# A four-layer graph network: layer 1's input and the small rows turned by VectorE and DRAM instead of TensorE, one statistics instruction per norm, and a mask kept in DRAM

## The chip, the cores and the metric

The kernel runs on one core of one Trainium2 chip. The metric is the device time of one execution in microseconds (us). A core has TensorE (PE, matrix products), VectorE (DVE), ScalarE (ACT), GpSimd (POOL) and SyncE (SP), which issues all DMAs here; 16 DMA engines carry them out. Every engine works through its own instructions in the order in which the program has them.

## The reference, cut to what matters

There are 64 independent graphs of N = 256 nodes with D = 256 features, and everything is float32. Four layers follow each other, and around each is a residual and a layer norm over the features:

```python
x = _layernorm(x + _L0_gnn_ref(x, adj, ...))   # 4 heads, sigmoid(q k^T) * adj, degree-normed; own layer norm
x = _layernorm(x + _L1_gnn_ref(x, adj, ...))   # 8 heads, softmax(where(adj > 0, q k^T / sqrt(32), NEG))
x = _layernorm(x + _L2_gnn_ref(x, adj, ...))   # (adj @ x + eps x) W1 + b1, rmsnorm, silu, W2 + b2  (hidden 1024)
x = _layernorm(x + _L3_gnn_ref(x, adj, ...))   # Wh = x W; softmax(where(adj > 0, leaky(s1_i + s2_j), NEG)) Wh
                                               # own layer norm, gelu
```

In layer 1, q = x Wq + bq, k = x Wk + bk, v = x Wv + bv. In layer 2, the rms norm multiplies every token's hidden row by rsqrt(mean(h^2) + 1e-6). In layer 3, s1 and s2 are Wh times the two halves of the vector a. The biases bq and bk are inputs (they hold zeros).

## The kernel before, in words

**Tiling.** A graph's 256 x 256 array is one tile of 128 partitions by 512 words: two halves n of 128 tokens each, side by side. A product that sums over features needs its operand feature-major (features on the partitions), so x has to be transposed between layers.

**A planner sets the order.** `graph` records each step of one graph as an operation with an engine, a cost, the values that it reads and writes, and for ACT work that needs a function table a turn. `Plan.order` then lays out all 64 graphs at once, picking at every step the operation that can start first by the costs written in the code, with the buffer slots of `SLOTS` as a limit. Turns go round by round: in a round the sigmoid of one graph's layer 0 is done, then the exponentials of layers 1 and 3 of older graphs, then the silu of layer 2, then the gelu of layer 3. `ROUND = 0, 2, 5, 7` says how many rounds later a graph's layer 1, 2 and 3 have their turn, and `TAIL` presses the last graphs together. So at any moment some eight graphs are under way, and PE takes matmuls of one graph while others wait for DVE, ACT or a DMA. The order that comes out is fixed in the program.

**PE's three ways of working.** Most matmuls use the whole array (mode `full`). The scores of layers 0 and 1 (L502, L582) use it in `rows`, the weighted sums of these layers and two small sums over partitions (L542, L618, L520, L680) in `columns`, so that several small products run side by side. `CHANGE` lists what the planner reckons for a change of mode. With `JOINT = 8, 58` the small sum of one graph's layer 2 (L680, columns) is joined to the first scores of another graph's layer 1 (L582, rows) in the middle rounds.

**Two ways to transpose a tile.** `transposed` (L323) uses four PE transposes of 128 x 128 into PSUM, and `copy` (L359, ACT) brings the result to SBUF. `far_transposed` uses DVE's transpose of 32 x 32 blocks (L335), writes the result to DRAM and reads it back so that the blocks land where they belong. With `in_order=True` that is four DMAs of 64 KB out (L341, pieces of 512 B) and four back (L345, pieces of 128 B); otherwise it is one of 256 KB out (L349) and four back (L351). Layer 0's result, layer 3's input (`xT3`) and layer 3's weights (`eT3`) go this way, except for the first or last few graphs (`NEAR`); layer 1's weights have a version of their own (L603, L605, L607). Layer 1's input `xT` goes through PE for every graph.

**Small rows.** A value per token that sits on the partitions has to be laid along the free axis, for all partitions alike, in three places. For layer 1's reciprocals r, PE transposes them (L625), ACT copies them (L627), and they go out to DRAM and come back spread over the partitions (L628, L631). For layer 2's rms factor, `rs` is computed on POOL (L688) and PE transposes a broadcast column into PSUM (`pr`, L693, two transposes). For layer 3's s2 the same is done from `v3` (L731).

**Norms.** `stats` takes a mean and variance per token with one `bn_stats` for each half n (L393) and one `bn_aggr` for each (L395); POOL then adds eps and takes the power -1/2 (L405, L406). There are six such norms per graph.

**Masks.** `masked` (L476) turns `adj` into 0 or NEG with one DVE pass. Layers 1 and 3 each load `adj` (L315) and each mask it.

Of the kernel before, what the change touches and what calls it, by code (L numbers as in the profile page):

```python
# [29 lines left out]
WORDS = {"s": 516, "d": 1024, "b": 2048, "c": 32, "p": 512, "h": 1024}  # L30
# [6 lines left out]
JOINT = 8, 58  # L37

ROUND = 0, 2, 5, 7
TAIL = 0, 1, 3, 4  # L40
SLOTS = {"s": 42, "d": 10, "b": 3, "c": 72, "p": 8, "h": 8}
# [41 lines left out]
class Plan:  # L83
# [61 lines left out]
    def order(self):  # L145
# [3 lines left out]
        for op in reversed(self.ops):  # L149
            op.due = min((nxt.due for nxt in op.after), default=4 * (min(op.graph + ROUND[3], self.graphs - 1 + TAIL[3]) + 1))  # L150
            if op.turn is not None:
                op.due = min(op.due, op.turn)
# [74 lines left out]
def weights(plan, nc, c, t):  # L227
# [15 lines left out]
    def row(name, key, n=D):  # L243

        v = const(name, [P, n])
        op("SP", 470, lambda: nc.sync.dma_start(
            v.t, bass.AP(tensor=t[key].tensor, offset=t[key].offset, ap=[[0, P], [1, n]])), [v], after=3500, size=n // 2)
# [12 lines left out]
    column("b1_q", "L1_gnn_bq"), column("b1_v", "L1_gnn_bv"), row("b1_o", "L1_gnn_bo")  # L260
# [3 lines left out]
    row("g3", "L3_gnn_gamma"), row("b3", "L3_gnn_beta"), row("a3", "L3_gnn_a", 2 * D)  # L264
# [17 lines left out]
    op("DVE", 400, lambda ps=ps, v=v: nc.vector.tensor_tensor(v.t, ps.t[:, :D], c.b1_o.t, OP.add), [v], [ps, c.b1_o])  # L282
# [15 lines left out]
def graph(plan, nc, c, t, out, b):  # L298
# [10 lines left out]
    def turn(layer, func):  # L309
        return 4 * min(b + ROUND[layer], plan.graphs - 1 + TAIL[layer]) + func  # L310
# [20 lines left out]
    def far_transposed(src, name, in_order=True):  # L331


        eb, far, dst = Value("s", "eb"), Value("h", "far", 4), Value("s", name, 4)
# [3 lines left out]
        if in_order:  # L338
            F = lambda a: far.t[:64].rearrange("(a z) (y w) -> a (z y) w", a=4, w=P)[a]
            for a in range(4):  # L340
                op("SP", 470, lambda a=a: nc.sync.dma_start(  # L341
                    F(a).rearrange("(b j) w -> j b w", b=4),
                    eb.t[32 * a:32 * a + 32].rearrange("j (b w) -> j b w", b=4)), [(far, a)], [eb], after=2400, size=64)
            for a in range(4):
                op("SP", 655, lambda a=a: nc.sync.dma_start(  # L345
                    dst.t.rearrange("q (g a i) -> a q g i", g=4, a=4)[a],
                    F(a).rearrange("q (g i) -> q g i", g=4)), [(dst, a)], [(far, a)], after=2200, size=200)
            return dst
        op("SP", 470, lambda: nc.sync.dma_start(far.t[:, :512], eb.t), [(far, i) for i in range(4)], [eb], after=2900, size=256)  # L349
        for q in range(4):  # L350
            op("SP", 470, lambda q=q: nc.sync.dma_start(  # L351
                dst.t[32 * q:32 * q + 32].rearrange("j (a g) -> j a g", a=4),
                far.t[:, :512].rearrange("(a j) (b g) -> b j a g", a=4, b=4)[q]), [(dst, q)],
                [(far, i) for i in range(4)], after=1900, size=64)
# [32 lines left out]
    def stats(src, r=None):  # L387


        mv, st = Value("c", "mv", 2), Value("c", "st", 2)  # L390
        m = lambda: mv.t[:, :6].rearrange("p (n k) -> p n k", n=2)
        for n in range(NB):
            op("DVE", 328, lambda n=n: dve.bn_stats(st.t[:, 6 * n:6 * n + 6], two(src)[:, n, :]), [(st, n)], [(src, n)])  # L393
        for n in range(NB):
            op("DVE", 82, lambda n=n: dve.bn_aggr(m()[:, n, 0:2], st.t[:, 6 * n:6 * n + 6]), [(mv, n)], [(st, n)])  # L395

        r2 = lambda: r.t[:, :NB]
        if r:
            def fn():
                for _ in range(2):  # L400
                    dve.tensor_tensor(m()[:, :, 1], m()[:, :, 1], r2(), OP.mult)
            op("DVE", 250, fn, [mv], [mv, r])

        def fn():
            pool.tensor_scalar(m()[:, :, 2], m()[:, :, 1], 1e-5, None, op0=OP.add)  # L405
            pool.tensor_tensor(m()[:, :, 2], m()[:, :, 2], c.mhalf[:, :NB], OP.pow)  # L406
        op("POOL", 1010, fn, [mv], [mv], after=580)
        if r:
            op("DVE", 60, lambda: dve.tensor_tensor(m()[:, :, 2], m()[:, :, 2], r2(), OP.mult), [mv], [mv, r])
        return mv, m  # L410

    def normed(src, name):
        mv, m = stats(src)
        dst = Value("s", name, 2)
        if name != 'o' or b >= plan.graphs - ENDS:
            op("DVE", 70, lambda: dve.scalar_tensor_tensor(  # L416
                m()[:, :, 0], m()[:, :, 0], -1.0, m()[:, :, 2], op0=OP.mult, op1=OP.mult), [mv], [mv])
        for n in range(NB):
            if name != 'o' or b >= plan.graphs - ENDS:
                op("ACT", 492, lambda n=n: act.activation(  # L420
                    two(dst)[:, n, :], two(src)[:, n, :], AF.Identity, bias=m()[:, n, 0:1], scale=m()[:, n, 2:3]),
# [3 lines left out]
                two(dst)[:, n, :], two(src)[:, n, :], m()[:, n, 0:1], m()[:, n, 2:3],  # L425
# [13 lines left out]
    def affine(y, mv, m, g, add, r=(), src=None):  # L439

        if src and b >= plan.graphs - ENDS:
            op("DVE", 70, lambda: dve.scalar_tensor_tensor(
                m()[:, :, 0], m()[:, :, 0], -1.0, m()[:, :, 2], op0=OP.mult, op1=OP.mult), [mv], [mv])
            for n in range(NB):
                op("ACT", 491, lambda n=n: act.activation(
                    two(y)[:, n, :], two(src)[:, n, :], AF.Identity, bias=m()[:, n, 0:1], scale=m()[:, n, 2:3]),
# [5 lines left out]
        for n in range(NB):  # L452
            op("DVE", 395, lambda n=n: dve.scalar_tensor_tensor(
                two(y)[:, n, :], two(src)[:, n, :], m()[:, n, 0:1], g.t, op0=OP.subtract, op1=OP.mult),
                [(y, n)], [(src, n), mv, g])
            op("DVE", 395, lambda n=n: dve.scalar_tensor_tensor(
                two(y)[:, n, :], two(y)[:, n, :], m()[:, n, 2:3], add(n), op0=OP.mult, op1=OP.add),
                [(y, n)], [(y, n), mv, *r])

    def softmax(logits, negmask, scale, e, E, part, r, col, when):  # L460


        low = Value("c", "low", 2)
        for n in range(NB):
            op("DVE", 345, lambda n=n: dve.tensor_tensor_reduce(  # L465
                out=E(n), in0=two(logits)[:, n, :], in1=two(negmask)[:, n, :], scale=-scale,
                scalar=3.0e38, op0=OP.add, op1=OP.min, accum_out=low.t[:, n:n + 1]),
                [(e, part(n)), (low, n)], [(logits, n), (negmask, n)])
# [368 lines left out]
```

## Time and profile before

| | |
|---|---|
| time, three runs | 2696.25, 2698.45, 2700.91 us; median 2698.45 us |
| span of the profiled execution | 2698.6 us, granted TensorE clock 0.997 |
| PE busy | 2666.0 us (99%) |
| DVE busy | 2436.7 us (90%) |
| ACT busy | 2228.8 us (83%) |
| POOL busy | 588.5 us (22%) |
| DMA | 497.40 MB on SP's queue in 707744 packets, 67.0% of the 16 engines' time |
| SP | 3578 DMA issues, 1755 us of issuing |

The span runs from the first to the last instruction of the profiled execution. It is 0.15 us over the median of the runs, so that sums made against the span stand for the median as well. A matmul's busy time in the profile reaches past the start of the next one, since matmuls are pipelined; what a matmul costs PE is therefore read from the step between two starts in the timeline, not from its busy time. A DMA packet is one contiguous piece that one DMA engine moves, or the 4 B that tell a semaphore of its end.

### The profile page before, as it was taken

To read this page: it belongs to the slowest core of one execution; us is meant where nothing else is said; L and a number is where in the kernel's file an instruction comes from. 1 tells how busy PE (TensorE), PEld (TensorE's weight loads), DVE (VectorE), ACT (ScalarE), POOL (GpSimd) and SP (SyncE) were. 2 spreads that over 40 slices of the span, in tenths; PEclk is the share of its full clock that TensorE was granted. 3 is DMA by queue.
4 is the path that set the end of the run, shared out by engine and by line. 5 is a ranking of instruction groups with operands and counts; after the bars stand their busy time and mean duration, and the time that the engine had idled before them with its cause. 6 is when DMAs were issued, how large, how long until landed. Compare 5 with 4: busy or idle time off the path is not lost.

```text
span 2698.6 us, 56499 instructions
## 1 busy us (share of the span) xinstructions
PE 2666.0 (99%) x17568; PEld 2144.9 (79%) x17568; DVE 2436.7 (90%) x7480; ACT 2228.8 (83%) x5343; POOL 588.5 (22%) x902
## 2 busy tenths in 40 slices
PE   8999999999999999999999999999999999999997
PEld 6777788887887878878888878888788788787776
DVE  6789999999899999999999999989999899999986
ACT  4888888888888988888888888888888888888886
POOL 1111222212222212222222222222222222222212
PEclk9999999999999999999999999999999999999999
DMA  4476875766767767667767677677676676776661
GB/s 146 133 213 176 219 219 161 211 192 183 200 185 187 215 178 189 196 181 207 202 169 206 186 190 212 173 190 201 172 213 193 169 212 189 186 212 181 169 173 36
DMA packets 708045, 501.01 MB, mean 186 GB/s; under 512 B 309792, under 2 KB 667552, under 8 KB 707744
## 3 DMA queue, kind: packets, MB, share of 16 engines
q1 hardware_dynamic: 707744, 497.40, 67.0%
q8 instruction: 140, 2.29, 0.4%
q14 instruction: 161, 1.32, 0.2%
HBM read 301.35 MB, written 195.82 MB: 184 GB/s over the span
## 4 chain that ended last, share of the span: by engine, by line
PE 93%; DVE 3%; ACT 2%; DMA 1%; SPq 1%; issue 1%; POOL 0%; ACTq 0%; POOLq 0%; DVEq 0%
PE ps L368 16%; PE ps L707 16%; PE ps L661 16%; PE ps L379 15%; PE ps L582 5%; PE ps L502 4%; PE ps L542 4%; PE av L618 4%; PE ps L722 4%; PE ps L649 4%; PE ps L323 1%; PE ps L520 1%; PE pr L693 1%; DVE e L465 1%; PE ps L731 0%
## 5 line engine op out<-in xcount | busy, mean ns | idle before, releaser
L470 ACT ACTIVATE e<-e,low 128x256 f32<-128x256 f32 x1152 | 574.6, 500 | 83.7 <-DVE low L465 82.9
L707 PE MATMUL ps<-w,hT 128*128 128x256 f32 x2048 | 466.8, 380 | 1.3 <-ACT hT L699 1.2
L661 PE MATMUL ps<-aggT,w 128*128 128x256 f32 x2048 | 463.4, 380 | 1.6 <-ACT aggT L359 1.0
L707 PEld LDWEIGHTS ps<-w,hT 128*128 128x128 f32 x2048 | 385.7, 190 | 60.4 <-issue 4.6
L661 PEld LDWEIGHTS ps<-aggT,w 128*128 128x128 f32 x2048 | 383.3, 190 | 57.0 <-issue 2.8
L405 POOL TENSOR_SCALAR mv<-mv 128x2 f32<-128x2 f32 x384 | 127.8, 333 | 1316.8 <-DVE mv L395 888.0
L465 DVE CUSTOM_DVE_ANT_0 e<-ps,adj 128x256 f32<-128x256 f32 x1024 | 361.7, 418 | 30.0 <-PE ps L582 29.9
L406 POOL TENSOR_TENSOR mv<-mv,mhalf 128x2 f32<-128x2 f32 x384 | 306.0, 797 | 32.0
L603 DVE STREAM_TRANSPOSE eb<-e 128x1024 f32<-128x1024 f32 x248 | 300.8, 1221 | 0.8 <-ACT e L470 0.7
L668 ACT ACTIVATE hT<-ps,br,r 128x256 f32<-128x256 f32 x512 | 255.7, 585 | 33.9 <-PE ps L707 30.6
L393 DVE BATCH_NORM_STATS2 st<-y 128x6 f32<-128x256 f32 x640 | 238.3, 408 | 1.2
L420 ACT ACTIVATE x<-y,mv 128x256 f32<-128x256 f32 x384 | 215.2, 600 | 28.9 <-DVE mv L416 26.1
L666 ACT ACTIVATE sq<-ps,b 128x256 f32<-128x256 f32 x512 | 220.0, 474 | 20.2 <-PE ps L661 19.7
L470 ACT ACTIVATION_READ_ACCUMULATOR e<-e,low 128x1 f32 x1152 | 219.0, 190 | 0.0
L508 DVE TENSOR_TENSOR att<-att,adjT 128x512 f32<-128x512 f32 x256 | 166.4, 676 | 10.0 <-ACT att L506 10.0
L688 POOL TENSOR_TENSOR rs<-rs,mhalf 128x2 f32<-128x2 f32 x64 | 45.6, 712 | 540.4 <-DVE rs L686 518.9
L528 POOL TENSOR_TENSOR dp<-dp,mhalf 128x8 f32<-128x8 f32 x64 | 110.2, 1722 | 215.8 <-DVE dp L527 168.3
L697 DVE TENSOR_TENSOR hT<-hT,pr 128x1024 f32<-128x1024 f32 x128 | 150.0, 1210 | 5.2 <-PE pr L693 4.3
L582 PE MATMUL ps<-kT,qT 32*128 32x256 f32 x2048 | 146.2, 399 | 0.0
L673 DVE TENSOR_TENSOR sq<-sq 128x512 f32<-128x512 f32 x192 | 129.5, 675 | 11.1 <-ACT sq L666 10.2
L368 PE MATMUL ps<-x0T,w_q 128*128 128x256 f32 x512 | 130.4, 385 | 6.6 <-DMA x0T<-in_xT 6.6
L506 ACT ACTIVATE att<-ps 128x512 f32<-128x512 f32 x256 | 132.2, 603 | 3.8 <-PE ps L502 3.1
(119 smaller groups left out, 5508.9 us busy)
## 6 DMA issues: line engine op xcount, KB each, us to landing
far<-eb SPq DMA_DIRECT2D x248, 512.0 KB, 3.6
eT<-far SPq DMA_DIRECT2D x992, 128.0 KB, 4.1
adj<-in_adj SPq DMA_DIRECT2D x128, 256.0 KB, 5.1
far<-eb SPq DMA_DIRECT2D x488, 64.0 KB, 2.0
x0T<-in_xT SPq DMA_DIRECT2D x64, 256.0 KB, 4.7
adjT<-in_adjT SPq DMA_DIRECT2D x64, 256.0 KB, 4.9
x<-in_x SPq DMA_DIRECT2D x64, 256.0 KB, 5.2
adj<-in_adjT SPq DMA_DIRECT2D x64, 256.0 KB, 4.8
```

Source lines behind the costliest of these rows:

```text
L368: pe.matmul(two(ps)[:, o, :], w.t[:, k, o * P:(o + 1) * P], two(xT)[:, k, :], start=(k == 0), stop=(k == DB - 1))
L379: pe.matmul(two(ps)[:, n, :], two(xT)[:, k, n * P:(n + 1) * P], w()[:, k, :], start=(k == 0), stop=(k == DB - 1))
L393: op("DVE", 328, lambda n=n: dve.bn_stats(st.t[:, 6 * n:6 * n + 6], two(src)[:, n, :]), [(st, n)], [(src, n)])
L406: pool.tensor_tensor(m()[:, :, 2], m()[:, :, 2], c.mhalf[:, :NB], OP.pow)
L465: op("DVE", 345, lambda n=n: dve.tensor_tensor_reduce(out=E(n), in0=two(logits)[:, n, :], in1=two(negmask)[:, n, :], scale=-scale, scalar= ...
L470: op("ACT", 491, lambda n=n: act.activation(E(n), E(n), AF.Exp, bias=low.t[:, n:n + 1], scale=-1.0, accum_out=r.t[:, col(n):col(n) + 1]), ...
L582: pe.matmul(two(pss[i])[:, n, :], two(qT1)[s, hq, n * P:(n + 1) * P], two(kT1)[s, hq, :], start=True, stop=True)
L603: op("DVE", 1155, lambda e=e, eb=eb: dve.transpose(eb.t.rearrange("p (b g i) -> p g b i", b=4, i=32), e.t.rearrange("p (g b i) -> p g b i" ...
L661: pe.matmul(two(ps)[:, i, :], c.w2_1.t[:, k, (j + i) * P:(j + i + 1) * P], two(aggT)[:, k, :], start=(k == 0), stop=(k == DB - 1))
L666: op("ACT", 357, lambda ps=ps, sq=sq, i=i, j=j: act.activation(two(sq)[:, i, :], two(ps)[:, i, :], AF.Square, bias=c.b2_1.t[:, j + i:j + i ...
L668: op("ACT", 491, lambda ps=ps, i=i, j=j: act.activation(Hb(j + i)[:, 0], two(ps)[:, i, :], AF.Identity, bias=c.br2.t[:, j + i:j + i + 1], ...
L707: pe.matmul(two(ps)[:, n, :], Hb(j)[:, 0, n * P:(n + 1) * P], c.w2_2.t[:, j, :], start=(j == 0), stop=(j == HB - 1))
```

## The change

1. Layer 1's input goes through `far_transposed` from the second graph on (`NEAR[0]` = 1), so that PE's four transposes and ACT's copy fall away there.
2. `far_transposed` in order is now one DMA out of 2048 pieces of 128 B and four back of 512 pieces of 128 B each, instead of four out in pieces of 512 B and four back.
3. The small rows are turned by DVE's 32 x 32 transpose and go through DRAM: r (a 128 x 32 tile; it now holds the row minima too), the rms factor and s2 (a 128 x 64 tile each, by the new `over_partitions`, not for the last three graphs). What used them reads them with a permuted pattern (four runs of 32).
4. `stats` is one `bn_stats` over both halves, reading them word by word in turn; it keeps count, mean and count times variance of the even and of the odd words, which are the two halves. There is no `bn_aggr`.
5. Layer 1's mask is written to DRAM (`keep`) and layer 3 reads it, instead of loading and masking `adj` again.
6. Layer 1's k has its bias added as q's has (two ACT passes of 256 words for one copy of 512). Layer 2's rms product and silu are cut by token half instead of by hidden half; `adj2`'s two additions become one; `yT`'s one product becomes two; the rms eps moves from DVE to POOL.
7. `JOINT = 99, 0`: no joint operations. `ROUND` gives layer 3 to round 8 instead of 7; there are other slots.

```diff
-JOINT = 8, 58
-ROUND = 0, 2, 5, 7
+JOINT = 99, 0
+ROUND = 0, 2, 5, 8, 8
...
-            for a in range(4):
-                op("SP", 470, lambda a=a: nc.sync.dma_start(
-                    F(a).rearrange("(b j) w -> j b w", b=4),
-                    eb.t[32 * a:32 * a + 32].rearrange("j (b w) -> j b w", b=4)), [(far, a)], [eb], after=2400, size=64)
-            for a in range(4):
-                op("SP", 655, lambda a=a: nc.sync.dma_start(
-                    dst.t.rearrange("q (g a i) -> a q g i", g=4, a=4)[a],
-                    F(a).rearrange("q (g i) -> q g i", g=4)), [(dst, a)], [(far, a)], after=2200, size=200)
+            F = lambda: far.t[:64].rearrange("(b g r) (p i) -> b g (r p) i", b=4, g=4, i=32)
+            op("SP", 470, lambda: nc.sync.dma_start(
+                F().rearrange("b g p i -> p (b g) i"), eb.t.rearrange("p (g i) -> p g i", i=32)), [far], [eb], after=3300, size=400)
+            for q in range(4):
+                op("SP", 470, lambda q=q: nc.sync.dma_start(
+                    dst.t[32 * q:32 * q + 32].rearrange("j (g i) -> j g i", i=32),
+                    F()[q].rearrange("g (a j) i -> j (g a) i", a=4)), [(dst, q)], [far], after=2200, size=100)
...
+    def over_partitions(src, at):
+        far, dst = Value("f", "far"), Value("w", "row")
+        op("SP", 470, lambda: nc.sync.dma_start(far.t, src.t), [far], [src], after=2000, size=32)
+        op("SP", 470, lambda: nc.sync.dma_start(
+            dst.t.rearrange("p (a m) -> p a m", a=4),
+            far.t.rearrange("(a c) m -> c a m", a=4)[at][None].to_broadcast([P, 4, 64])),
+            [dst], [far], after=2300, size=200)
+        return dst
...
-        for n in range(NB):
-            op("DVE", 328, lambda n=n: dve.bn_stats(st.t[:, 6 * n:6 * n + 6], two(src)[:, n, :]), [(st, n)], [(src, n)])
-        for n in range(NB):
-            op("DVE", 82, lambda n=n: dve.bn_aggr(m()[:, n, 0:2], st.t[:, 6 * n:6 * n + 6]), [(mv, n)], [(st, n)])
+        op("DVE", 640, lambda: dve.bn_stats(mv.t[:, :6], src.t.rearrange("p (n c) -> p c n", n=NB)), [mv], [src])
...
+    keep = Value("m", "keep")
+    op("SP", 470, lambda negmask=negmask: nc.sync.dma_start(keep.t, negmask.t), [keep], [negmask], after=3000, size=256)
-    xT = copy(transposed(x), "xT")
+    xT = copy(transposed(x), "xT") if b < NEAR[0] else far_transposed(x, "xT")
...
-    ps = Value("p", "ps")
-    op("PE", PE_TR, lambda ps=ps: pe.transpose(ps.t[:16, :P], r.t[:, :16], c.ident), [ps], [r], mode="transpose")
-    op("ACT", 160, lambda ps=ps: act.copy(rT.t[:16, :P], ps.t[:16, :P]), [rT], [ps])
+    op("DVE", 95, lambda: dve.transpose(rT.t, r.t), [rT], [r])
...
+        back = Value("t", "back")
+        op("DVE", 125, lambda: dve.transpose(back.t, rs.t), [back], [rs])
+        pr, by = over_partitions(back, 0), "p (a n i) -> p n a i"
...
+        op("DVE", 125, lambda: dve.transpose(turned.t.rearrange("p (n k) -> p n k", n=NB), V3()[:, :, D - 30:]), [turned], [v3])
+        s2, by3 = over_partitions(turned, 31), "p (a n i) -> p n a i"
...
-    negmask = masked(load("adj3", "adj"))
+    op("SP", 470, lambda: nc.sync.dma_start(negmask.t, keep.t), [negmask], [keep], after=5000, size=256)
```

Counted over the two programs, the instructions on PE, with two halves of a float32 product as one, become 560 transposes fewer (252 of x, 122 for the rms factor, 122 for s2, 64 of r) and otherwise stay. PE goes from the whole array into rows or columns 338 times instead of 254.

## The prediction

> **What bounds the kernel now.** I read the page first: its busy row, the slices and the chain.
>
> ```profile
> span 2698.6 us, 56499 instructions
> PE 2666.0 (99%) x17568; PEld 2144.9 (79%) x17568; DVE 2436.7 (90%) x7480; ACT 2228.8 (83%) x5343; POOL 588.5 (22%) x902
> PE   8999999999999999999999999999999999999997
> PE 93%; DVE 3%; ACT 2%; DMA 1%; SPq 1%; issue 1%; POOL 0%; ACTq 0%; POOLq 0%; DVEq 0%
> ```
>
> PE is busy in every slice and is 93% of the chain that ended last. Two of the longest waits of PE show how little is left between its instructions; the first is the start of the program, and all after it add up to some 10 us:
>
> ```profile
> PE ps L368 <- DMA x0T<-in_xT: 6.6, 1, 6.6
> PE ps L379 <- ACT eT L359: 1.6, 1, 1.6
> ```
>
> So time is PE's instruction stream, and a PE instruction is worth its step, from its start to the next one's. The timeline shows the steps (start, duration, count):
>
> ```profile
> 1197.85 1.03 PE L368 MATMUL ps<-x0T,w_q 128*128 128x256 f32 x4
> 1198.71 1.03 PE L368 MATMUL ps<-x0T,w_k 128*128 128x256 f32 x4
> 1199.67 0.32 PE L680 MATMUL ps<-sq,mean_of 128*32 128x64 f32 x8
> 1199.92 1.15 PE L582 MATMUL ps<-kT,qT 32*128 32x256 f32 x16
> 1201.00 0.28 PE L625 MATMUL ps<-ident,r 128*16 128x128 f32 x1
> 1201.11 1.03 PE L649 MATMUL ps<-adj,x 128*128 128x256 f32 x4
> ```
>
> Four full matmuls step 0.86 us (1197.85 to 1198.71), 216 ns each; the next four take 0.96 before a column product starts: entering rows or columns costs 93 ns. The transpose L625 is busy 0.28 but steps only 0.11. Over the whole trace these medians hold: 109 ns a transpose (159 for the first of an L693 pair, 114 for L625), +93 ns for entering; leaving costs 109 ns after L582 (1.076 us for its 16, 0.967 where a second such group follows) and 113 after L618, L520 and L680; after L542 and L502 nothing shows. With every operation at its median step, the stream before sums to 2639 us. The rest of 2698.6 is 6.6 before the first matmul, 16 after the last one's start and 37 of waits and jitter. The span stands 0.15 us over the median of the runs, so no correction is made.
>
> **PE, step by step.** Removed: 252 transposes of x by 109 ns = 27.5; 61 pairs for the rms factor by 109 + 159 = 16.3; 122 for s2 by 109 = 13.3; 64 of r by 114 = 7.3. Sum 64.4 us. Against it stands the order: the transposes and the joint operations were also bridges out of rows and columns. Counted over both orders, PE enters from the whole array 338 times for 254: 84 x 93 ns = +7.8. Exits that cost: L618 52 for 18 (+3.8), L520 50 for 62 (-1.4), L680 51 for 61 (-1.1), L582 128 for 124 (+0.4), together +1.7. Net: -64.4 + 7.8 + 1.7 = **-54.9 us**.
>
> **DVE** (90% busy, so it could take PE's place). The rows:
>
> ```profile
> L393 DVE BATCH_NORM_STATS2 st<-y 128x6 f32<-128x256 f32 x640 | 238.3, 408 | 1.2
> L395 DVE BATCH_NORM_AGGREGATE mv<-st 128x2 f32<-128x6 f32 x768 | 115.7, 165 | 0.0
> L335 DVE STREAM_TRANSPOSE eb<-x 128x512 f32<-128x512 f32 x61 | 42.7, 700 | 2.8 <-ACT x L420 2.6
> L685 DVE STREAM_TRANSPOSE sq<-ps 128x64 f32<-128x64 f32 x64 | 15.6, 243 | 5.4 <-PE ps L680 5.2
> L476 DVE TENSOR_SCALAR adj<-adj 128x512 f32<-128x512 f32 x128 | 52.6, 411 | 0.4 <-DMA adj<-in_adj 0.3
> ```
>
> Statistics lose 238.3 + 48.6 (the PSUM form) + 115.7 = 402.6 and gain 384 passes over 512 words. No row reads words from two places 1 KB apart in turn; one-word-per-cycle passes over 512 words take 670 to 700 ns here, 256 words 400 to 410. I take 675 (259 us); the dear end is double the slope, 675 + 270 = 945 ns (+104 us); 600 is the cheap end (-29). So -143. The other edits: one mask pass fewer -26; L686 gone -10; one `adj2` addition fewer -5; x's block transpose 63 x 0.70 = +44; the three small transposes 64 x 0.2 + 122 x 0.243 = +43 (r's is half as wide as the 243 ns row); `yT` in two +9. L697's product takes its row from SBUF in runs of 32 instead of from PSUM; I leave its 1.21 us, since L335 reads runs of 32 at one word per cycle. DVE: 2437 - 88 = 2349 us, 89% of the new span: its share hardly moves. ACT: x copies -37, r copies -16, the split of k +17: 2193, 83%. POOL gains 64 x 333 ns = 21, in a chain with 40 us of other graphs' work beside it. All three lie beside PE and count nothing so long as they stay under it.
>
> **DMA** is where the change pays. The rows before:
>
> ```profile
> q1 hardware_dynamic: 707744, 497.40, 67.0%
> far<-eb SPq DMA_DIRECT2D x488, 64.0 KB, 2.0
> xT<-far SPq DMA_DIRECT2D x244, 64.0 KB, 2.5
> ```
>
> The packets by size (count, mean time): 249856 of 128 B, 12.9 ns; 95744 of 512 B, 31.5; 262016 of 1 KB, 60.1; 8192 of 2 KB, 88.9; 32000 of 4 KB, 175; 59937 semaphore packets of 4 B, 10.4. Over 16 engines that is 1824 us. The change: 516096 more of 128 B (three tiles per graph in 2048 pieces each way) = +416; 143616 of 256 B (rows spread over partitions) at 19.1, on the line between the 128 B and 512 B rows = +171; 63488 fewer of 512 B = -125; 32768 fewer of 1 KB = -123; 16384 more of 2 KB (the kept mask) = +91; semaphores +3. Sum +433: 2257 us, **85% of the new span** for 67%. Of the 128 B packets 378880 are writes to DRAM, and every 128 B packet before is a read. Write and read differ little where both exist (512 B: 33.6 and 30.0; 1 KB stores and loads both 46 undisturbed), so I take 12.9; the dear end is the 512 B write's 33.6, the cheap end, undisturbed packets of all sizes at their medians, 1985 us in all.
>
> The Trainium skill (DMA: Bandwidth & Descriptors, section Specifications) speaks against this edit: below 512 B a DMA engine does read-modify-write. The trace's short reads do not show it and it has no short data write. If each such write cost double, the DMAs would hold some 2560 us, 97%, as near to a bound as PE.
>
> **SP's queue** issues in order and had 1755 us of 2698.6 in issuing. A DMA of 128 pieces takes 432 ns, of 512 pieces (L345) 623. Out go 488 + 244 + 244 issues and 64 `adj` loads (566 us); in come 185 writes of 2048 pieces (0.62 to 1.39 us each, the latter on the line through both rows), 740 reads at 0.62, 128 of the mask, 244 of the rows: 720 to 880. So 1910 to 2070, 72 to 78%: no bound. The writes of `eb` and of `keep` wait on DVE, and behind them on SP stand the loads and reads of other graphs: that is the wait added.
>
> **Chains.** x to `xT` was 1.0 us (four transposes and ACT's 0.59) and becomes 0.70 + 0.43 + 2.0 + 4 x 0.62 + 2.5 = 8.1 us by the rows. What hides the 7 us more is about 41 us of PE per graph from older graphs, L661 and L707 above all; uncovered it would cost 63 x 7 = 440. The rms factor and s2 grow by some 5 us each, under the same cover. In the tail layer 3 of five graphs instead of four falls in the last round: PE is idle 21 us after 2400 us now, 5 per graph, so +5 (0 to 15).
>
> **Sum.** 2698.6 - 54.9 + 5 = 2648.7, so **2649 us**, with the 37 us of waits and jitter unchanged.
>
> **Rivals.** (1) Forecast, PE stays the bound: 0.70, own range 2613 to 2686. The low end drops all but 6 of the 37 us and the tail's 5, since every engine's sum falls; the high end adds another 37. (2) The gain turns into waits on longer round trips behind SP: for it, 185 waiting writes in one queue where L341 already waits 135 us for DVE; against it, waits of SP of that kind do not reach PE now. At 0.65 us per graph that is 42 us: 2690. 0.12, about half of it faster, the rest even between same and slower. (3) **Slower: short DRAM writes.** At 33.6 ns a piece the DMAs hold 2257 + 378880 x 20.7 / 16 ns = 2747 us; at 97% full, no better than PE manages, 2830 us. It decides from the price at which 97% of the forecast is full: (2569 - 2257) x 16 / 378880 = 13 ns more, 26 ns a piece; from 28 ns it is slower than before. For it: twice the short packets, most of the new ones writes. Against: the 512 B rows. 0.13. (4) Alternating reads make `bn_stats` 945 ns: DVE 2453 us, 93%, as full as its steady windows are now (92 to 93%), so PE waits a little more: 2670. 0.05.
>
> **Numbers.** About 0.2% is what a measurement of this kernel can tell from no change. Faster: 0.70 + 0.06 + 0.04 = 0.80; same 0.04; slower 0.03 + 0.13 = 0.16. The range takes in (1), (4) and most of (2), 2613 to 2703; only (3) and some of (2) stay out.
>
> **What would show it.** Right: PE at 98% or more, about 17000 PE records, steps of 216 ns, waits of PE under 60 us in sum, DMA near 85%, DVE near 89%, `bn_stats` near 675 ns. Wrong: DMA slices at 9 throughout with 128 B packets above 26 ns and PE waiting for `xT`, `xT3` or `eT3` by DMA (rival 3); PE waiting on DMAs at a moderate DMA share with SP solid (rival 2); `bn_stats` near 945 with PE waiting for DVE (rival 4). If a chain of waits stands on POOL, I have overlooked a path.

## The result and the profile after

| | before | after |
|---|---|---|
| time, median | 2697.67 us (2696.25 to 2700.91, four runs) | 3283.53 us (3276.59 to 3292.55, four runs) |
| ratio | | 1.2174, 95% interval 1.2152 to 1.2196 |
| span of the profiled execution | 2698.6 us | 3282.3 us |
| granted TensorE clock | 0.997 | 0.933 |

The forecast was 2649 us, 2613 to 2703. The time lies 635 us above it, far outside the range and on the other side. The page of the changed kernel (busy row, three of the slice rows, the DMA queue, the chain):

```profile
PE 2840.2 (87%) x17008; PEld 2196.2 (67%) x17008; DVE 2429.1 (74%) x6449; ACT 2218.5 (68%) x5279; POOL 599.6 (18%) x966
PE   8989888888888989789889879898979798988877
PEclk9999899999989999999999999899989898998988
DMA  5677666686767767777877767676867676777752
q1 hardware_dynamic: 1291968, 567.73, 69.1%
PE 29%; DMA 25%; DVE 15%; SPq 10%; ACT 5%; issue 3%; POOL 0%; DVEq 0%; ACTq 0%; POOLq 0%
DMA row<-far 10%; PE ps L390 6%; PE ps L731 5%; DMA eT<-far 5%; PE ps L676 5%; PE ps L379 4%; DMA far<-eb 3%; SPq L346 3%; DVE e L474 2%; SPq L620 2%; PE ps L664 2%; DMA yT<-far 2%; PE ps L594 2%; SPq L641 2%; DVE mv L403 2%
```

No resource is full: every engine's share has fallen, PE idles everywhere, and the DMA engines are busy 69% of the span, less than the 85% that was forecast. A chain with PE at 29% (93% before) says that work waits for round trips, and its largest single link is a DMA, `row<-far`. These are the reads of L362 that spread the rms factor and s2 over the partitions. The waits on DVE, ACT and PE (us in sum, times, longest) say who waited:

```profile
DVE hT L720 <- DMA row<-far: 244.1, 58, 8.2
ACT e L764 <- DMA row<-far: 223.0, 44, 10.5
PE ps L390 <- DMA eT<-far: 53.4, 16, 8.3
PE ps L746 <- DMA xT<-far: 36.1, 14, 5.3
```

The two consumers of the rows, one on DVE and one on ACT, wait 4 to 5 us at a time. PE itself waits for quite different things, in many places (162 us for DMAs, 137 for ACT, 125 for DVE): it is last in line. The DMA view points to the reason (KB, median us from issue to landing):

```profile
row<-far SPq DMA_DIRECT2D x122, 128.0 KB, 8.6
eT<-far SPq DMA_DIRECT2D x992, 128.0 KB, 4.0
```

A `row` read moves no more bytes than an `eT` read and takes twice as long. In it all 128 partitions read the same four pieces of 256 B from DRAM. The timeline of SP shows what can then happen to the queue (start, duration):

```profile
1551.63 0.38 SPq L362 DMA_DIRECT2D row<-far  x1
1552.20 0.36 SPq L641 DMA_DIRECT2D rb<-far  x1
1552.76 0.38 SPq L362 DMA_DIRECT2D row<-far  x1
1553.27 0.41 SPq L343 DMA_DIRECT2D far<-eb  x1
1553.72 6.75 SPq L641 DMA_DIRECT2D rb<-far  x1
```

The row reads are issued in 0.38 us, but two issues later one small issue holds SP for 6.75 us, and with it every load and read of the other graphs. (The issue just ahead of it, L343, is a write of 2048 pieces, so the row reads are not the only candidate.) Counted over the trace, SP issues for 2425 us (1910 to 2070 were forecast), and 150 issues take over 2 us (3 before), the longest 9.8. Of these 150, 45 come within four issues after a row read, where 17 would fall by chance; 101 come within four issues after a write of 2048 pieces, to which the experiments return.

For PE a second tally is used below: over all steps from one PE start to the next, what lies above 216 ns in steps longer than 330 ns is called **stall**. Before it was 19 us, after 621 us. 173 us of these belong to steps without a gap, 168 of them at a halved clock. The granted clock stood at 0.5 in 77 stretches, 441 us together (20 us before); in the 8 us ahead of such a stretch PE had stood idle for 4.3 us in the mean, against 1.0 us in any 8 us of the run.

### The profile page after: what moved, and what is told of

Read it like the earlier page. It is cut to its first block, busy times and chain, and to the rows that moved or that the text cites. A ratio compares the mean times of both kernels' runs of the same rounds, so it can differ in the third digit from the quotient of the medians.

```text
span 3282.3 us, 55301 instructions
## 1 busy us (share of the span) xinstructions
PE 2840.2 (87%) x17008; PEld 2196.2 (67%) x17008; DVE 2429.1 (74%) x6449; ACT 2218.5 (68%) x5279; POOL 599.6 (18%) x966
## 4 chain that ended last, share of the span: by engine, by line
PE 29%; DMA 25%; DVE 15%; SPq 10%; ACT 5%; issue 3%; POOL 0%; DVEq 0%; ACTq 0%; POOLq 0%
DMA row<-far 10%; PE ps L390 6%; PE ps L731 5%; DMA eT<-far 5%; PE ps L676 5%; PE ps L379 4%; DMA far<-eb 3%; SPq L346 3%; DVE e L474 2%; SPq L620 2%; PE ps L664 2%; DMA yT<-far 2%; PE ps L594 2%; SPq L641 2%; DVE mv L403 2%
## 5 line engine op out<-in xcount | busy, mean ns | idle before, releaser
L479 ACT ACTIVATE e<-e,r 128x256 f32<-128x256 f32 x1024 | 511.8, 502 | 88.5 <-DVE r L474 85.8
L731 PE MATMUL ps<-w,hT 128*128 128x256 f32 x2048 | 504.7, 398 | 23.4 <-ACT hT L723 23.2
L720 DVE TENSOR_TENSOR hT<-hT,row 128x1024 f32<-128x1024 f32 x122 | 145.1, 1222 | 244.1 <-DMA row<-far 244.1
L764 ACT ACTIVATE e<-row,v 128x256 f32<-128x256 f32 x122 | 57.7, 503 | 252.6 <-DMA row<-far 223.0
L403 DVE BATCH_NORM_STATS2 mv<-y 128x6 f32<-128x512 f32 x320 | 219.1, 690 | 2.2
L594 PE MATMUL ps<-kT,qT 32*128 32x256 f32 x2048 | 176.7, 429 | 48.0 <-ACT kT L580 20.9
L746 PE MATMUL ps<-w,xT 128*128 128x258 f32 x512 | 151.6, 446 | 63.9 <-DMA xT<-far 36.1
L390 PE MATMUL ps<-v,eT 128*128 128x256 f32 x512 | 148.5, 440 | 64.1 <-DMA eT<-far 53.4
L479 ACT ACTIVATION_READ_ACCUMULATOR e<-e,r 128x1 f32 x1024 | 197.3, 193 | 0.0
L594 PEld LDWEIGHTS ps<-kT,qT 32*128 32x128 f32 x2048 | 109.3, 197 | 105.8 <-issue 26.4
L537 POOL TENSOR_TENSOR dp<-dp,mhalf 128x8 f32<-128x8 f32 x64 | 109.9, 1717 | 382.8 <-DVE dp L536 375.5
```

The lines of the kernel that those rows point to most:

```text
L390: pe.matmul(two(ps)[:, n, :], two(xT)[:, k, n * P:(n + 1) * P], w()[:, k, :], start=(k == 0), stop=(k == DB - 1))
L403: op("DVE", 640, lambda: dve.bn_stats(mv.t[:, :6], src.t.rearrange("p (n c) -> p c n", n=NB)), [mv], [src])
L479: op("ACT", 491, lambda n=n: act.activation(E(n), E(n), AF.Exp, bias=L(n), scale=-1.0, accum_out=r.t[:, col(n):col(n) + 1]), [(e, part(n)) ...
L594: pe.matmul(two(pss[i])[:, n, :], two(qT1)[s, hq, n * P:(n + 1) * P], two(kT1)[s, hq, :], start=True, stop=True)
L731: pe.matmul(two(ps)[:, n, :], Hb(j)[:, 0, n * P:(n + 1) * P], c.w2_2.t[:, j, :], start=(j == 0), stop=(j == HB - 1))
```

## The experiments

Unless said otherwise a ratio is against the kernel before on the same chip, with its 95% interval. The first kernels keep the order of the changed kernel, so that only the DMAs differ.

**The rows' reads, same order.** `spread`: every partition reads its own 256 B four times, so that the row no longer holds the factors. `onepiece`: the row lies in one piece of 1 KB, and all partitions read that.

```diff
 # spread
-            far.t.rearrange("(a c) m -> c a m", a=4)[at][None].to_broadcast([P, 4, 64])),
+            far.t[:, None, :].to_broadcast([P, 4, 64])),
 # onepiece
+            far.t.rearrange("(c a) m -> a c m", a=4), src.t), ...
+            dst.t, far.t.rearrange("(c a) m -> c (a m)", a=4)[at][None].to_broadcast([P, 256])),
```

> Theory A: the row read (row<-far) is slow because 128 partitions read the same four 256 B pieces of DRAM and these reads are served one after another; the DMA engines stand meanwhile and all DMAs queued behind wait. This kernel is the changed one in the same order with as many packets of the same size, except that each partition reads its own 256 B row four times (its rows therefore hold other values than the reference's). A: row<-far lands in about 3 us instead of 8.6, and the time falls by most of 122 x 4 to 5 us, to 2650 to 2800. Theory B: the short packets and the longer chains through DRAM cost the time whatever they read; then row<-far stays above 7 us and the time within 3% of 3283. Theory C: the planner's order is bad by itself (no joint operations, layer 3 a round later): also about 3283.

> The changed kernel in the same order, but the row is stored so that each of the 128 partitions reads one piece of 1 KB instead of four of 256 B: the same bytes, read as often, in a quarter of the packets. If the hot place serves requests (A1), row<-far lands in 3 to 4 us and the time falls to 2750 to 2850. If it serves bytes (A2), it still lands in 7 to 9 us and the time stays within 5% of 3283. Theory B: under 2% better than 3283, since 47000 packets of 1.3 million go.

`spread`: 2828.76 us, 1.0485 (1.0454 to 1.0515). `onepiece`: 2854.75 us, 1.0581 (1.0535 to 1.0628). The work, the bytes and the order are those of the changed kernel; only where `spread`'s partitions read has changed, and 455 us are gone. In `spread` (the DMA view, the busy row and the line of DVE's consumer):

```profile
row<-far SPq DMA_DIRECT2D x122, 128.0 KB, 3.1
PE 2679.2 (95%) x17008; PEld 2103.0 (74%) x17008; DVE 2418.9 (86%) x6449; ACT 2209.4 (78%) x5279; POOL 623.6 (22%) x966
L720 DVE TENSOR_TENSOR hT<-hT,row 128x1024 f32<-128x1024 f32 x122 | 144.3, 1215 | 13.6 <-DMA row<-far 13.5
```

A row lands in 3.1 us instead of 8.6, DVE waits 13.5 us for it instead of 244.1, and PE's stalls are 177 us. A quarter as many requests to one place (`onepiece`) does nearly as well.

**The read by itself.** `probe` leaves out the network: 12 times each, a 128 KB load of some kind and behind it a plain load from another place.

> Only DMAs, one after another, twelve of each form, each with a plain 128 KB load of x right behind it; nothing of the reference is computed, the output is a copy of x. Read is the time to landing. A: plain rows of 1 KB 2 to 3 us; hot_all (128 partitions read the same four 256 B pieces, as the change does) 5 us or more, hot_half about half of its excess, hot_quarter a quarter; own_rows (as many packets, each partition its own row) about as plain; the load behind hot_all is late by as much as hot_all itself; with four and sixteen copies of the row, near plain. hot_pieces tells requests from bytes: 2 to 3 us or as hot_all. B: hot_all lands within 1 us of own_rows. scattered_out against plain_out (256 KB in 2048 pieces of 128 B, or 128 of 2 KB) is the price of short writes: within 1 us of each other if they cost 13 ns a piece, 2.5 us later or more if they cost 33.

Its timeline (SP's issues, the kind of read named by its tile):

```profile
21.47 0.32 SPq L57 DMA_DIRECT2D plain<-wide  x1
22.37 0.33 SPq L39 DMA_DIRECT2D behind_plain<-in_x  x1
23.54 0.32 SPq L57 DMA_DIRECT2D plain<-wide  x1
...
35.35 0.37 SPq L42 DMA_DIRECT2D hot_all<-far  x1
35.77 0.50 SPq L39 DMA_DIRECT2D behind_hot_all<-in_x  x1
43.19 0.37 SPq L42 DMA_DIRECT2D hot_all<-far  x1
```

SP gets ahead of the DMAs only so far, so the time from one issue of a kind to the next is what one pair of loads takes: from `plain` to `plain` 2.07 us, from `hot_all` to `hot_all` 7.84. The median periods are:

| read of 128 KB (fewer KB for 64, 32 partitions) | requests to one place | us |
|---|---|---|
| `plain`; `own_rows` | none | 2.04; 2.13 |
| `hot_all`: 128 partitions, 4 pieces each | 512 | 7.85 |
| `hot_half`: 64 partitions | 256 | 4.94 |
| `hot_quarter`: 32 partitions | 128 | 2.94 |
| `hot_pieces`: 128 partitions, one piece of 1 KB | 128 | 3.03 |
| `copies_four`: four DMAs of 32 partitions, each from a row of its own | 128 to each of four | 2.33 |

What counts is the number of requests to the shared place, not the bytes: 128 requests take about as long with 32 KB (`hot_quarter`) as with 128 KB (`hot_pieces`), and the same 512 requests spread over four rows take 2.33 us. 512 cost 5.8 us more than `plain`, 256 cost 2.9, 128 cost 0.9 to 1.0. The packet records show it directly: within a read of `hot_all`, `hot_half` or `hot_quarter` the packets of 256 B start 12 ns apart in the mean, in `own_rows` 1.5 ns. Nor does one DMA engine do all the work: the 4 B packets of a `hot_all` read and of the plain load behind it, 32 for 16 engines, come together at the end (65.3 to 67.1 us, then 73.0 to 74.8), and none of them early. The plain loads between take turns with the hot ones in one queue, so they come once in 7.84 us as well. `copies_sixteen`, sixteen small DMAs, takes 5.83 us: SP needs that long for its 17 issues of 0.34 us. A write of 2048 pieces of 128 B takes 3.04 us where a plain write of the same bytes takes 2.03.

**The row reads alone on the kernel before.** `hot_alone` takes only the rms factor and s2 through DRAM; it leaves out the permuted reading, so the values stand at other tokens.

> The kernel before with the row reads alone: rms factor and s2 by DVE and DRAM, read by all 128 partitions from one place (their consumers take the row in the order in which it lies, so the values stand at other tokens). Theory A: each read holds the DMA engines for 5.8 us longer than a plain one, 122 of them 700 us; before, the DMAs are idle for a third of the time, 880 us, so part is hidden: 2950 to 3250, and row<-far lands in 7 to 10 us. If it needs the change's other DMAs to hurt: under 2850.

3207.39 us, 1.1886 (1.1863 to 1.191): +509 us, from an edit that takes 29.6 us of transposes off PE (16.3 and 13.3 in the prediction's sum). So the row reads need no other part of the change to cost this much. The longer chain of the rows is part of it too; the same kernel with reads from separate places was not run. Held issues are not needed either: only 38 issues take over 2 us here, 112 us together. The consumers wait for the landing itself, 9.1 us:

```profile
ACT e L755 <- DMA row<-far: 297.1, 53, 8.2
DVE hT L712 <- DMA row<-far: 217.3, 58, 6.8
```

**A mend with the right values.** `copies`: the same order; the write puts 16 copies of the row's pieces into DRAM, and 8 partitions read each copy in one piece of 1 KB. `copies_rb` also has r's row read in pieces of 1 KB instead of 256 B.

```diff
+            far.t[:64].rearrange("(k a) m -> a k m", a=4),
+            src.t.rearrange("(a c) m -> c a m", a=4)[at][:, None, :].to_broadcast([4, 16, 64])), ...
+            dst.t, far.t[:64].rearrange("(k a) m -> k (a m)", a=4)[:, None, :].to_broadcast([16, 8, 256])),
```

> The changed kernel in the same order and with the same number of DMAs, but the four pieces that make up the row are written to DRAM sixteen times, and each copy is read by eight partitions in 1 KB pieces (64 + 128 packets instead of 128 + 512). Theory A (reads of one place are served one after another): the row read lands in 2.5 to 3 us, the time is that of the kernel whose partitions read their own rows, 2829, or up to 30 us less for the packets saved. B (the row's cost is its packets): the same, so this run only says whether the repair holds with the right values; if it stays above 2850, something else than the place is slow.

> The copies kernel in the same order, with r's row stored in token order, by one DMA as in the change, so that its eight reads fetch 1 KB pieces (32 each) again instead of 128 pieces of 256 B. T1 (the remaining reads of one place): 40 to 100 us less than the copies kernel, as a quarter-size hot read took 0.9 us longer than a plain one. T4 (SP's in-order queue): within 15 us of it, since SP issues as many DMAs.

2832.42 us, 1.0497 (1.0475 to 1.0518), and 2829.37 us, 1.0486 (1.0465 to 1.0507). So 451 us come back with a layout of the same row, and r's short pieces are no part of the rest. The rest is some 130 us over the kernel before, and PE stalls 184 us in `copies`: a second cause.

**No rows.** `rows_pe`: the rms factor and s2 by PE for all graphs, and the order planned anew. `rb_pieces` is the same order with r's row in 1 KB pieces, at the price of four writes for one.

```diff
-    if b >= plan.graphs - NEAR[2]:   # both places
+    if True:
```

> The changed kernel with the rms factor and s2 turned by PE for all graphs, as before; the rest of the change stays (layer 1's input, r's row, statistics, mask, no joint operations). The planner orders it anew. A: no slow row read is left, and the time is near what the prediction's sum gives with 30 us of transposes put back, 2660 to 2720. B: layer 1's input and the 128 B pieces still cost, above 3000. C: also above 3000.

> What is still 100 us over the time before, once the rms factor and s2 are back on PE (2801 us)? This kernel is that one in the same planned order, but r's row is stored so that its eight reads fetch pieces of 1 KB again, as before the change, instead of four of 256 B for each of 32 partitions (three more small writes per graph pay for it). T1, the remaining same-place reads: a quarter-size hot read took 0.9 us more than a plain one in the DMA-only run, eight per graph, so up to 7 us per graph are freed: 2720 to 2750, rb<-far lands in 1.9 us instead of 2.4. T2 (2048-piece transposes load the DMAs and block SP) and T3 (the planner's landing times are too short for the new DMAs): within 15 us of 2801.

2801.47 us, 1.0384 (1.0306 to 1.0461), and 2901.08 us, 1.0755 (1.0734 to 1.0777). Without any row the kernel is still 104 us slower than before. (The two runs of `rows_pe` lie 17 us apart, so its differences from others are good to some ten us.) `rb_pieces` answers another question than it was made for: it adds 192 issues, SP's issuing grows by 112 us (1995 to 2107), and the time by 100. That suggests that an issue on SP is no longer free in this kernel; but the row's four writes must also all land before it is read, and the two were not separated.

**SP's load and the planner's costs.** `act_loads` issues 320 input loads from ACT. `replan` tells the planner landings as they were measured (4.5 us for 3.3 and so on). `order3` and `far_order` tell it that DMAs move a KB in 3 and 2.5 ns instead of 4, so that it puts matmuls that need them earlier.

> The rows_pe kernel (2801 us) in the same order, with its 320 input loads issued by ACT instead of SP. T4, SP's queue is what ends last once the hot rows are gone (adding 192 small writes to it, 132 us of issuing, cost 100 us): SP loses some 200 us of issuing, PE's waits on DMA eT and xT shrink from 46 us to under 20 and the time falls to 2720 to 2770, though ACT gains some 140 us. T2 (DMA load alone): within 20 us of 2801. It can also get slower, above 2830, if ACT's own work then waits behind loads for free buffers.

> The rows_pe kernel with nothing changed but what the planner is told of landings: 4.5 us for the 2048-piece write, 3.5 for its reads and layer 0's, 4.0 and 3.0 for r's row, close to what was measured at the upper half (mean 4.1 and 3.0, 3.0, 3.7 and 2.7). The instructions are the same, in another order. T3: PE's waits fall from 117 us to under 60 and the time to 2700 to 2745. T1 and T2: within 20 us of 2801, since the DMAs hold as much.

> The repaired change (copies_rb, 2829 us) with one constant of the planner altered: it reckons 3 ns instead of 4 for each KB that a DMA is charged. The same instructions and DMAs in another order. T6, the planner's charges for the new DMAs (2.5 MB reckoned per graph row by row, in pieces that are charged more than their bytes) make it hold matmuls back, so that holes are in the order itself: PE's waits fall from about 180 us to under 100 and the time to 2690 to 2760. T2 and T4 (the DMAs or SP's queue themselves): 2810 to 2850, or more, as reads are now expected too early.

`act_loads` 2999.41 us, 1.1116 (1.1094 to 1.1138), although SP issues for 279 us less (1717 against 1995). PE now waits 158 us for DMAs (50 in `rows_pe`), 106 of them for `xT<-far`, and 31 us for ACT (22). ACT's own issues are held for 1.5 us at most, so a load stuck in ACT's order does not show as the reason; why the reads come late here was not found. `replan` 2796.0 us, 1.0366 (1.0341 to 1.0391), as `rows_pe`: the landings told are not the cause. `order3`, which is `copies_rb` with that one figure altered, 3032.75 us, 1.1236 (1.1219 to 1.1253): the charge was not too high; when PE is sent to the data earlier it stalls for 372 us instead of 178.

**The DMA form.** `far_old`: `rows_pe` with the in-order transposes in four DMAs out and four back again. `far_order` is this kernel with 2.5 ns a KB.

> The rows_pe kernel with the in-order transposes through DRAM in their old form (four DMAs out in 512 B pieces, four back), for layer 1's input too; the planner orders it anew with the old costs. T2: the 2048-piece writes are the cause; PE's waits fall from 117 us to under 50 and the time to 2700 to 2740, although SP issues 555 DMAs more. T3: 2750 to 2800, as the old form's landing times fit the old costs only in part. T1: no change, 2790 to 2810.

> The far_old kernel (2772 us: rms factor and s2 by PE, transposes through DRAM in the old form) with the planner reckoning 2.5 ns per charged KB instead of 4. T6: 2690 to 2740. T2/T4: within 20 us of 2772.

2771.95 us, 1.0277 (1.0253 to 1.0301): 30 us less than `rows_pe` although SP has 555 more issues. SP's issues show what differs: with the one write of 2048 pieces 75 issues take over 2 us, 205 us together, and 70 of the 75 come within four issues after such a write (14 by chance); in the old form 7 do, 16 us. It is no more than a part of the second cause: the 2700 to 2740 us expected if these writes were all of it were missed. `far_order` is 2907.73 us, 1.0773 (1.0755 to 1.0791), as `order3`.

**Layer 1's input alone, and the statistics alone,** on the kernel before. `x_later` is `x_alone` with layer 3's turn one round later.

```diff
-    xT = copy(transposed(x), "xT")
+    xT = copy(transposed(x), "xT") if b < NEAR[0] else far_transposed(x, "xT")
 # x_later
-ROUND = 0, 2, 5, 7
+ROUND = 0, 2, 5, 8
```

> The kernel before with one part of the change alone: layer 1's input through DVE and DRAM, in the old form with pieces of 512 B. PE loses 252 transposes (-27.5 us) and enters rows or columns 317 times for 254 (+6 for entering, +7 for leaving), DVE gains 44 us (92%). The prediction's way of summing gives 2698 - 15 = 2683, 2670 to 2695. If the longer chain and 504 more DMA issues turn into waits, 2710 to 2780.

> The x_alone kernel (2893 us) with layer 3's turn a round later, as the change has it; nothing else. T5, the cover of the longer chain of layer 1's input is gone in the old round plan, since what it delays pushes the later layers against their turns: 2750 to 2810. T4, SP's 2051 us of issuing or the DMAs: within 25 us of 2893.

> The kernel before with one part of the change alone: one statistics instruction per norm. By the prediction's sum it takes 143 us off DVE (2437 to 2294) and nothing off PE, whose steps make the time: 2685 to 2700, same as before within 0.5%. If DVE's 90% were what holds PE back, 2640 to 2680.

`x_alone` 2893.45 us, 1.073 (1.0711 to 1.0748); `x_later` 2782.39 us, 1.0311 (1.0291 to 1.0332); `stats` 2722.81 us, 1.0096 (1.0079 to 1.0113). The trip of x through DRAM costs 196 us in the old round plan, and one round more for layer 3 takes 111 of them back (that round without the trip was not run). PE's waits in `x_alone`, the three largest:

```profile
PE ps L542 <- DVE v L534: 22.5, 6, 5.5
PE ps L707 <- ACT hT L699: 21.2, 12, 3.8
PE ps L379 <- DVE yT L635: 20.8, 10, 5.3
```

None of them is for `xT`. I read this so: a graph that arrives late in layer 1 is late in every layer after it, and PE meets the delay there. That `x_later` is 111 us faster fits; no run follows one graph through.

**What is left of the change.** `x_by_pe` is `far_old` with x by PE as before; `far_rounds` is `far_old` with layers 1 and 2 one round later.

```diff
 # x_by_pe
-    xT = copy(transposed(x), "xT") if b < NEAR[0] else far_transposed(x, "xT")
+    xT = copy(transposed(x), "xT")
 # far_rounds
-ROUND = 0, 2, 5, 8, 8
+ROUND = 0, 3, 6, 8, 8
```

> far_old (rms factor and s2 by PE, old form of the DVE transposes with eight DMAs) with layer 1's input transposed by PE again, as before. PE gains 252 transposes of 109 ns: 27 us. Theory A (the longer path of x is what makes PE wait in far_old, 86 us of waits over the steps): the waits fall to the 20 to 30 us of the kernel before, PE's steps rise from 2655 to some 2682, and the time is about 2735 us. Theory B (the waits come from the other parts that are left, the kept mask, r by DVE, one-instruction statistics, no joint operations): the waits stay near 86 us and the time is about 2800 us.

> far_old with layers 1 and 2 one round later (ROUND 0, 3, 6, 8, 8 for 0, 2, 5, 8, 8), the work itself unchanged, so that a graph has one round more between layer 0's end and layer 1's turn, where x makes its trip through DRAM. Theory A (the trip of x is too long for the two rounds between): about half of the 86 us of waits go, some 2730 us. Theory B (DMAs are late because SP's queue issues them late, wherever the turn is): within 10 us of far_old's 2772 us. Layer 2 has one round less before layer 3; if that is the tighter place the time rises instead.

`x_by_pe` 2726.64 us, 1.0111 (1.0096 to 1.0126); `far_rounds` 2737.11 us, 1.0147 (1.013 to 1.0164). The chains of `x_by_pe` and then of `far_rounds`:

```profile
PE 90%; DVE 4%; ACT 2%; DMA 2%; SPq 1%; issue 1%; POOL 0%; POOLq 0%; DVEq 0%; ACTq 0%
```

```profile
PE 80%; DVE 9%; DMA 4%; SPq 3%; ACT 2%; issue 2%; POOL 1%; DVEq 0%; ACTq 0%; POOLq 0%
```

With x by PE the stalls are 28 us (86 in `far_old`) and PE carries the chain again. With one round more for x the time is 35 us shorter for the same work, though here the tally of long steps falls only from 86 to 73 us; most of the rest is in shorter steps. `x_by_pe` also takes 504 issues off SP (2147 to 1763 us of issuing), which `far_rounds` leaves in place; that `far_rounds` gets back 35 us, with `x_by_pe` at 45, speaks for the trip's length and against SP's load. Both agree that the trip of x is the second cause. No kernel here is faster than the one before.

## Why the prediction was wrong

Of the 635 us between 2649 and 3283.5, 49 are the gain that was forecast and did not come. The other 586, from the kernel before to the changed one, come apart along the kernels, each step one edit or a group of them:

| step | time | difference |
|---|---|---|
| changed kernel | 3283.5 | |
| rows not read from one place (`spread`) | 2828.8 | -455 |
| rows by PE, new order (`rows_pe`) | 2801.5 | -27 |
| DMAs in the old form (`far_old`) | 2772.0 | -30 |
| x by PE (`x_by_pe`) | 2726.6 | -45 |
| kernel before | 2697.7 | -29 |

**The failed step: the price of the spread rows, and their cover.** The prediction priced them as packets, "143616 of 256 B (rows spread over partitions) at 19.1", and their chain as "some 5 us each, under the same cover". The packets did take 17.2 ns each, and the sum of all packet times is 2281 us against 2257. But the packet times do not hold the price: the DMA engines show as 69% busy while the DMAs are late. The price is in the landing, 8.6 us, and in what stands behind: from DVE's transpose to the row's landing 23.7 us pass in the mean (17.0 in `spread`), and DVE and ACT wait 467 us for rows, so the cover was not there. The trace of before held a hint, in rows that I had not put side by side:

```profile
rb<-far SPq DMA_DIRECT2D x512, 32.0 KB, 1.9
b_l<-in_L_gnn_b_lin SPq DMA_DIRECT2D x1, 128.0 KB, 5.2
```

Both spread one row. With 32 readers it lands in 1.9 us; the bias, with 128 readers of one piece each, in 5.2, where the `eT<-far` of the same 128 KB lands in 4.1. It is a hint and no more: the seven such rows of 128 KB land in 3.9 to 5.5 us, among the loads of weights, where a plain one of 256 KB takes up to 9.2. The change makes 122 DMAs of this kind, with four pieces for each reader. Taking the landing from such a line, and not from packets, would have shown a DMA to be tested alone; it would not have given 455 us.

**The second failed step: what hides x's 7 us.** "What hides the 7 us more is about 41 us of PE per graph": `x_alone` costs 196 us net, 3.1 us per graph, 44% of the 440 us given for no cover. PE's 41 us of older graphs are there on average, but the order is fixed by rounds and planned costs, and a step that is late by microseconds is met by PE at once. In the changed kernel's own rounds the same trip costs less: its removal gives 45 us, although PE then does 27.5 us of transposes more. So the waits that the trip brings there are worth some 72 us: the 27.5 that it was meant to save and 45 more.

The trip itself was mis-sized too. The sum gave it 8.1 us. In the changed kernel 22.9 us pass in the mean from the start of DVE's transpose to the landing of the last read (trips of layers 1 and 3, paired in order of issue): 0.7 in the transpose, 5.4 in the write, 5.5 in the reads, and 11.3 between data being ready and SP's issue of the next DMA. The sum had 2.0 for the write's landing, from a DMA of 64 KB, and nothing for the wait for SP's turn. `x_alone` has 14.4 us, and layer 3's trips in the kernel before, which the prediction could have measured, 11.8.

**PE's term.** The sum of steps without the stalls falls from 2657 us to 2628 in `spread`, 29 us of the 54.9. With x by PE (`x_by_pe`) it is 2671, 14 more than before; counted on its trace, the prediction's own prices give -7.3 for r's transposes and +6.1 for entries (338 for 254) and exits, together -1. So `spread` lacks 26 us of the gain and `x_by_pe` takes some 16 more than these prices give, all in steps under the tally's threshold. Short waits can make that difference; I did not separate them.

**DVE's term.** `bn_stats` over 512 words:

```profile
L403 DVE BATCH_NORM_STATS2 mv<-y 128x6 f32<-128x512 f32 x320 | 219.1, 690 | 2.2
```

690 ns for 675. Rival 4 (945 ns) is refuted. The busy times of DVE's rows in sum fall by 74 us (2841 to 2766) for the 88 forecast. The busy row falls by 8 only, from 2437 to 2429, since it counts overlapping instructions once: of the 127 us of `bn_aggr`, 61 had lain under what ran before them. I had taken a sum of row times off a busy time. In `stats` the 131 us fewer in the sum of DVE's rows bring nothing, as DVE did not bound, and the order that comes out is 1% slower: its stalls are 29 us (19 before) and its other steps 13 us longer, 4.7 of them by 51 more entries into rows or columns (305 for 254).

**SP's term.** 1910 to 2070 us "no bound" did not hold for the changed kernel (2425). `rows_pe` has 1995, but with 244 issues fewer, for which the same sum gives some 1805 to 1965. The estimate had the median of an issue; it left out that an issue can be held for 2 to 10 us by what was issued before it.

**The rivals.** (2), waits on longer round trips with SP solid and DMA moderate, is what happened, though only 162 of PE's 426 us of waits are for DMAs and the rest for ACT and DVE. It was given 0.12 and 42 us, and the row reads gave it ten times that. That x's trip costs 45 us from `x_by_pe` to `far_old` is close to the 42 by luck: the same trip costs 196 in `x_alone`. (3), short DRAM writes, is refuted as the cause: 128 B packets take 13.5 ns in the mean with the writes among them (12.9 before, reads alone), and the write of 2048 pieces by itself costs 1.0 us more than a plain one. The Trainium skill's rule (DMA: Bandwidth & Descriptors, section Specifications) that a DMA engine does read-modify-write below 512 B did not show as a price in these packets. The forecast (1) fell with the row reads; without them it would still have been wrong: `spread`, which has all of the change but the reads of one place, lies 180 us above it, on the slower side.

**Open.** What makes `x_by_pe` 29 us slower than the kernel before is not taken apart beyond `stats` (25 us alone). In `far_old` 6.4 of the trip's 16.2 us pass between data being ready and SP's issue (1.2 of 11.8 in the kernel before) and 9.0 in the write and the reads; how much of the 6.4 is the planned order and how much are held issues was not isolated.

## What to carry to other kernels

A DMA that gives one DRAM row to many partitions is priced by its number of requests to the same place, not by its bytes or its packets' times; look in the trace for a constant spread over all partitions and take its landing, or write the row several times and let few partitions read each copy. When PE is at 99%, moving a step off PE into a longer chain needs an order that gives the chain more room: one round more took the price of x's trip from 196 us to 85, and no run here made it pay. Test the chain alone first, and measure its whole trip, waits for the queue included, where the trace already has one like it. Do not subtract sums of instruction times from a busy row that counts overlaps once.

## What the runs showed of the hardware that I had not expected

- Reads of the same DRAM place by many partitions come one after another: their packets start 12 ns apart, against 1.5 ns where each partition reads its own row (512 requests: 7.85 us against 2.04), and the plain loads that take turns with them in the queue come no oftener. The DMA engines' busy share does not show it: it was lower (69%) than with reads from separate places (80.8% in `spread`).
- An issue on SP, 0.43 us in the median, can be held for long behind writes of 2048 pieces (over 2 us 70 times in `rows_pe`, within four issues after one; `far_old`, without them, has 7 in all) and behind such reads (in `hot_alone`, without these writes, 36 of the 38 over 2 us come within eight issues after a row read; 4.6 us at most). With both, in the changed kernel, the longest was 9.8 us.
- After PE paused its clock was lower: 0.933 granted in the changed kernel, with 77 stretches at 0.5, against 0.997 before. At the halved clock 168 us of the stalls were longer steps and not waits.
